# Layer 1's outputs and its feed forward in one set of pools, with one square root for four batches

## The chip, the cores and the metric

The kernel runs on one core of a Trainium2 chip. Its engines are PE (TensorE, matrix products and transposes), DVE (VectorE), ACT (ScalarE), POOL (GpSimd) and SP (SyncE, which issues the DMAs). Each engine takes its instructions in order; between engines they wait on semaphores. The metric is the device time of one execution in microseconds. Three executions of the kernel before took 2666.43, 2668.34 and 2669.78 us; the median is 2668.34.

## The reference, cut to what matters

The model is four layers of attention and feed forward on 4 x 1024 tokens of 128 features, each with a layer norm ahead and a residual sum behind. The change lies at the joint between layer 1's "attention" (a small network trained token by token, whose trained weights are then applied to all tokens) and layer 1's feed forward (eight experts with gates):

```python
def _layernorm(x, axis=-1, eps=1e-05):
    m = jnp.mean(x, axis=axis, keepdims=True)
    v = jnp.var(x, axis=axis, keepdims=True)
    return (x - m) / jnp.sqrt(v + eps)
...
    params, _ = jax.lax.scan(step, (W1, b1, W2, b2), (k, v))
    q = x @ W_Q
    return _mlp(params, q)                      # silu(q @ W1 + b1) @ W2 + b2
...
    gate_logits = jax.nn.softmax(x @ gate_w + gate_b, axis=-1)
    selected = (gate_logits >= THRESHOLD).astype(x.dtype)
    weights = gate_logits * selected
    wsum = jnp.sum(weights, axis=-1, keepdims=True)
    weights = weights / jnp.where(wsum == 0, jnp.ones_like(wsum), wsum)
    for e in range(E):
        out = out + weights[:, e:e + 1] * (x @ expert_w[e] + expert_b[e])
...
    x = x + _L1_attn_ref(_layernorm(x, axis=-1), ...)
    x = x + _L1_ffn_ref(_layernorm(x, axis=-1), ...)
    x = x + _L2_attn_ref(_layernorm(x, axis=-1), ...)
```

## The kernel before

All tokens stay in SBUF: `x` holds 32 tiles of 128 tokens by 128 features, four batches of eight tiles; `xnT` holds the normed tokens turned, features on the partitions. The layers run one after the other through one program; a scheduler orders the instructions of each engine by their dependencies and by the program's order, except in attention, which has an order written by hand. Tiles come from pools; a pool opened later is laid over the memory of one that has closed, and its tiles then wait until what was there is done with.

The stretch in question has these parts, in the program's order:

- `l1_attn` trains the small network (`l1_rounds`), and reads on every engine whether a slower path is to be taken (`tc.If`, line 681). Behind it opens the pools `l1o` and `l1q` and makes the outputs. First W_Q is turned and multiplied with W1 (`tp`, `wp`, `qw`), and the bias b2 is spread over the partitions (`b2p`, `bp`, `b2`). Then a loop of eight chunks of 512 tokens (lines 701 to 710): `hp`, one product with qw (L703); the Silu on ACT (L705); the bias added into x on POOL (`add_bias`, L169); `op`, four products with W2 (L709); and `op` added into x on DVE (`add_four`, L173). `hp` and `op` have two PSUM buffers each.
- `l1_ffn` opens its own pools: `ln` (f1l), `lps`, `one` (f1c), `two` (f1) and `ps`. It loads the experts' biases into `eb` with eight DMAs. Per batch it calls `ln_batch`, that is `ln_sums` (eight `bn_stats`, L134, and five small operations for sum and squares), `ln_moments` (the square root on ACT, L114, the reciprocal, and `nm`, L125) and `ln_scale` (xn on ACT, L154, and on POOL, L152, by turns; the transposes, L158; the copy into `xnT`, L164). `weights` makes the gates (L1014 and the small operations from L1019 to L1059), `biases` the weighted expert biases (L1065, L1070), `tile_of` the experts of one tile: two products of 512 columns (L1081, tile `ep`, three buffers), five multiply-adds on DVE (L1090), three scalings on ACT (L1088) and their sums on POOL (L1092).
- `l2_attn` begins with `layernorm(twice=...)`: the same steps with a second norm folded in, which takes more small operations for the root (lines 116 to 122, root at L123) and a scaled copy (L162). Its pool `ln` is laid over the memory in which f1l was. Attention's first products are L1205.

A function on ACT may need a table that is not loaded: the program then has an ACT_TABLE_LOAD ahead of it, at the same line. In the profile each f32 product shows as two matmul rows.

Of the kernel before, what the change touches and what calls it, by code (L numbers as in the profile page):

```python
# [27 lines left out]
class Net:  # L28
# [76 lines left out]
    def ln_moments(self, pool, b, twice=None):  # L105


        nc = self.nc
        if b not in self.ahead:
            self.ln_sums(pool, b)  # L110
        s, q = self.ahead.pop(b)
        rs = pool.tile([P, TPB], F32, tag="rs", name="rs")
        if twice is None:
            nc.scalar.activation(rs, q, AF.Sqrt, bias=self.eps, scale=1.0 / D)  # L114
# [12 lines left out]

    def ln_sums(self, pool, b):

        nc = self.nc  # L130

        st = pool.tile([P, TPB, 6], F32, tag="st", name="st")
        for i in range(TPB):
            nc.vector.bn_stats(st[:, i, :], self.x[:, b * TPB + i, :])  # L134
# [5 lines left out]
        nc.vector.tensor_add(q, q, d)  # L140
        nc.vector.tensor_add(s, st[:, :, 1], st[:, :, 4])
        self.ahead[b] = s, q
# [502 lines left out]
    def l1_attn(self):  # L645

        nc, tc = self.nc, self.tc
        wb1, wb2, wkv, wq = self.l1
        W1, B1 = wb1[:, 0:128], wb1[:, 128:129]
        W2, B2 = wb2[:, 0:128], wb2[:, 256:257]
        with ExitStack() as c_:
            one = c_.enter_context(tc.tile_pool(name="l1c", bufs=1))
            kT = one.tile([P, SEQ, NB], F32, tag="kT", name="kT")  # L660
            vT = one.tile([P, SEQ, NB], F32, tag="vT", name="vT")

            def project(bs, few, ln, lps, ps):
                by = [self.ln_moments(few, b) for b in bs]
                for b, m in zip(bs, by):
                    self.ln_scale(ln, lps, b, m)
                    for s in range(0, SEQ, 512):
                        for dst, cols in ((kT, slice(0, 128)), (vT, slice(128, 256))):
                            pp = ps.tile([P, 512], F32, tag="pp", name="pp")
                            nc.tensor.matmul(  # L670
                                pp, lhsT=wkv[:, cols], rhs=self.tok(b * TPB + s // P, 512), start=True, stop=True
                            )
                            if dst is kT:
                                nc.vector.tensor_copy(dst[:, s : s + 512, b], pp)
                            else:
                                nc.scalar.copy(dst[:, s : s + 512, b], pp)

            self.l0_ffn(project)
            bad = self.l1_rounds(one, kT, vT)
            many = nc.values_load(bad[0:1, 0:1], min_val=0, max_val=1)  # L680
            with tc.If(many > 0):
                self.l1_steps(kT, vT)
        with tc.tile_pool(name="l1o", bufs=2) as two, tc.tile_pool(name="l1q", bufs=2, space=PSUM) as ps:

            tp = ps.tile([P, D], F32, tag="one", name="tp", bufs=1)
            nc.tensor.transpose(tp, wq, self.ident)
            wqT = two.tile([P, D], F32, tag="wqT", name="wqT", bufs=1)
            nc.scalar.copy(wqT, tp)
            wp = ps.tile([P, D], F32, tag="one", name="wp", bufs=1)
            nc.tensor.matmul(wp, lhsT=wqT, rhs=W1, start=True, stop=True)  # L690
            qw = two.tile([P, D], F32, tag="qw", name="qw", bufs=1)
            nc.scalar.copy(qw, wp)
            b2p = ps.tile([1, D], F32, tag="two", name="b2p", bufs=1)
            nc.tensor.transpose(b2p, B2, self.ident)
            b2r = two.tile([1, D], F32, tag="b2r", name="b2r", bufs=1)
            nc.vector.tensor_copy(b2r, b2p)
            bp = ps.tile([P, D], F32, tag="two", name="bp", bufs=1)
            nc.tensor.matmul(bp, lhsT=self.ones[0:1, :], rhs=b2r, start=True, stop=True)
            b2 = two.tile([P, D], F32, tag="b2", name="b2", bufs=1)
            nc.vector.tensor_copy(b2, bp)  # L700
            for n in range(NB * SEQ // 512):
                hp = ps.tile([P, 512], F32, tag="hp", name="hp")
                nc.tensor.matmul(hp, lhsT=qw, rhs=self.tok(4 * n, 512), start=True, stop=True)  # L703
                a = two.tile([P, 512], F32, tag="a", name="a")
                nc.scalar.activation(a, hp, AF.Silu, bias=B1)  # L705
                self.add_bias(4 * n, b2)
                op = ps.tile([P, 4, D], F32, tag="op", name="op")
                for i in range(4):
                    nc.tensor.matmul(op[:, i, :], lhsT=a[:, i * P : (i + 1) * P], rhs=W2, start=True, stop=True)  # L709
                self.add_four(4 * n, op)  # L710

    def l1_rounds(self, keep, kT, vT):

# [316 lines left out]
    def l1_ffn(self):  # L1030


        nc, tc = self.nc, self.tc
        gw, gb, ew = self.f1
        E, OWN = 8, 5
        with ExitStack() as c:
            ln = c.enter_context(tc.tile_pool(name="f1l", bufs=2))
            lps = c.enter_context(tc.tile_pool(name="f1q", bufs=2, space=PSUM))
            one = c.enter_context(tc.tile_pool(name="f1c", bufs=2))
            two = c.enter_context(tc.tile_pool(name="f1", bufs=3))  # L1040
# [5 lines left out]
            ps = c.enter_context(tc.tile_pool(name="f1p", bufs=2, space=PSUM))  # L1046

            def weights(b):
                g = self.gates(one, ps, gw, gb, b * TPB, TPB)
                sel = one.tile([P, TPB, E], F32, tag="sel", name="sel")  # L1050
                nc.vector.tensor_scalar(sel, g, 0.1, None, ALU.is_ge)
                nc.vector.tensor_mul(g, g, sel)
                sm = one.tile([P, TPB], F32, tag="sm", name="sm")
                nc.vector.tensor_reduce(sm, g, axis=AX.X, op=ALU.add)
                z = one.tile([P, TPB], F32, tag="z", name="z")
                nc.vector.tensor_scalar(z, sm, 0.0, None, ALU.is_equal)
                nc.vector.tensor_add(sm, sm, z)
# [33 lines left out]
                for e in range(OWN, E):  # L1091
                    nc.gpsimd.tensor_add(xs, xs, sc[:, e - OWN, :])  # L1092

            self.ln_batch(ln, lps, 0)
            g = weights(0)
            for b in range(NB):
                if b + 1 < NB:
                    self.ln_batch(ln, lps, b + 1)
                biases(b, g)
                for i in range(TPB):  # L1100
                    tile_of(b * TPB + i, g[:, i, :])
                    if i == TPB // 2 and b + 1 < NB:
                        ahead = weights(b + 1)
                g = ahead
# [721 lines left out]
```

## Time and profile before

| what | us |
|---|---|
| median of three executions | 2668.34 |
| the profiled execution | 2665.29 |
| its span | 2663.6 |
| PE busy in the span | 2417.5 (91%) |
| DVE busy | 1795.2 (67%) |
| ACT busy | 1501.7 (56%) |
| POOL busy | 293.0 (11%) |
| outputs of layer 1, from the first `hp` to the last sum into x | 822.90 to 841.10 |
| feed forward of layer 1, to the last multiply on DVE | 841.10 to 945.70 |
| from there to attention's first product (L1205) | 945.70 to 956.30 |

The page of a profile has the busy time of each engine, the span in 40 slices with the clock that PE was granted, the DMA queues, the chain of waits that ended last, and the costliest groups of instructions. The timeline lists instructions by start, with duration, engine, line, operation, output and inputs, how many in a row ("x4"), and in brackets how long the engine had been idle and what released it. The windows give each engine's busy time in stretches. PEld is PE's loading of weights, which runs beside its products. Almost all DMA traffic of the stretch is the load of `eb`.

### The profile page before, as it was taken

The page shows a single profiled execution, that of the slowest core. Times are in us where ns is not written, and L with a number is a line of the kernel's source. Part 1 is how long each engine was busy: PE and PEld are TensorE (multiplying, and loading weights), DVE is VectorE, ACT ScalarE, POOL GpSimd, SP SyncE. Part 2 cuts the span into 40 slices and gives each one's busy share as a digit, 9 for nine tenths or more (in the row PEclk, how much of TensorE's full clock was granted, in tenths as well). Part 3 has the DMA queues.
Part 4 walks back from the last instruction along what each step waited for, and adds up shares of the span by engine and source line. Part 5 has one row for each costly group of instructions (what it writes and reads, how often), then busy time and mean ns, then how long its engine had stood idle before and what let it go on. Part 6 is the DMA issues. An engine that isn't in the chain of part 4 may idle for free.

```text
span 2663.6 us, 51041 instructions
## 1 busy us (share of the span) xinstructions
PE 2417.5 (91%) x19913; PEld 1222.1 (46%) x19913; DVE 1795.2 (67%) x3670; ACT 1501.7 (56%) x3333; POOL 293.0 (11%) x525
## 2 busy tenths in 40 slices
PE   5687758899997979999999779999999999999968
PEld 3455535699995333333333443333333333333356
DVE  5888877476764767776774357767767776777233
ACT  4466468455554434665566635666666566666632
POOL 6012021000002530000000440000000000000011
PEclk8699879899997989999999879999999999999969
DMA  1333320000000001001000000000000000000000
GB/s 45 74 77 74 73 74 1 1 1 1 1 1 2 1 9 18 14 15 18 14 14 6 5 5 10 9 10 8 8 9 12 8 9 10 8 8 8 3 18 18
DMA packets 116719, 46.66 MB, mean 18 GB/s; under 512 B 88473, under 2 KB 111097, under 8 KB 116474
## 3 DMA queue, kind: packets, MB, share of 16 engines
q1 hardware_dynamic: 116474, 43.35, 8.2%
q8 instruction: 159, 2.61, 0.4%
q14 instruction: 86, 0.70, 0.1%
HBM read 17.04 MB, written 12.98 MB: 11 GB/s over the span
## 4 chain that ended last, share of the span: by engine, by line
PE 57%; DVE 4%; ACT 1%; POOL 1%; issue 1%; SPq 0%; DMA 0%; POOLq 0%; DVEq 0%; ACTq 0%
PE pb L1319 32%; PE po L1341 16%; PE pa L1265 2%; DVE bm L1277 1%; PE pp L1205 1%; PE pv L1186 1%; DVE bm L1304 1%; PE tp L158 1%; PE gp L1014 1%; PE rp L1743 1%; DVE bm L1308 0%; PE pr L1598 0%; PE rp L1520 0%; PE ph L1756 0%; POOL sg L1753 0%
## 5 line engine op out<-in xcount | busy, mean ns | idle before, releaser
L1323 ACT ACTIVATE es<-pb 128x512 f32<-128x512 f32 x1536 | 836.3, 594 | 536.1 <-PE pb L1319 381.8
L1319 PE MATMUL pb<-q,k 32*128 32x512 f32 x3072 | 956.5, 641 | 3.9 <-DVE bm L1308 1.7
L1265 PE MATMUL pa<-k,q 32*128 32x512 f32 x2944 | 846.0, 650 | 10.4 <-DMA q<-q 10.3
L1277 DVE TENSOR_REDUCE bm<-pa 128x2 f32<-128x1024 f32 x496 | 605.0, 1225 | 261.1 <-PE pb L1319 168.0
L1341 PE MATMUL po<-es,v 128*32 128x256 f32 (+1 forms) x5760 | 480.0, 405 | 0.0
L1319 PEld LDWEIGHTS pb<-q,k 32*128 32x128 f32 x3072 | 313.5, 183 | 350.7 <-ACT es L1323 189.8
L1341 PEld LDWEIGHTS po<-es,v 128*32 128x32 f32 x5760 | 114.2, 108 | 543.1 <-issue 508.2
L1273 DVE TENSOR_REDUCE bm<-pa 128x16 f32<-128x1024 f32 x240 | 293.2, 1222 | 97.3 <-PE pb L1319 60.7
L1265 PEld LDWEIGHTS pa<-k,q 32*128 32x128 f32 x2944 | 234.4, 186 | 37.0 <-issue 18.6
L152 POOL TENSOR_SCALAR xn<-x,rs,nm 128x128 f32<-128x128 f32 x112 | 50.3, 464 | 1204.6 <-DVE nm L125 1026.9
L366 DVE TENSOR_TENSOR pr<-T,L 128x31 f32<-128x31 f32 (+15 forms) x248 | 92.0, 371 | 28.0 <-DMA L<-ld 20.7
L369 DVE TENSOR_TENSOR T<-T,pr 128x31 f32<-128x31 f32 (+15 forms) x248 | 93.1, 375 | 8.5
L1348 DVE COPY oT<-po 128x512 f32<-128x512 f32 x48 | 32.8, 682 | 95.6 <-PE po L1341 95.6
L158 PE MATMUL tp<-ident,xn 128*128 128x128 f32 x224 | 47.0, 361 | 42.7 <-ACT xn L154 38.1
L821 ACT ACTIVATE w<-tr,half 128x128 f32<-128x128 f32 x128 | 47.1, 368 | 48.3 <-PE tr L819 45.6
L796 ACT ACTIVATE a<-hp,wb 128x128 f32<-128x128 f32 x128 | 47.1, 368 | 41.6 <-PE hp L792 40.1
L1081 PE MATMUL ep<-L_ffn_expert_w,xnT 128*128 128x512 f32 x128 | 66.8, 654 | 3.3 <-DVE x L1090 3.1
L324 PE MATMUL wide<-bt,kt 32*128 32x128 f32 x512 | 29.9, 360 | 43.9 <-DVE mt L413 31.7
L486 PE MATMUL sp<-ux,kn 128*128 128x256 f32 x128 | 46.1, 493 | 17.7 <-ACT ux L475 17.7
L158 PEld LDWEIGHTS tp<-ident,xn 128*128 128x128 f32 x224 | 33.9, 179 | 61.2 <-ACT xn L154 47.0
L804 DVE TENSOR_TENSOR dlt<-gr,mask 128x128 f32<-128x128 f32 x96 | 28.0, 292 | 48.3 <-PE gr L802 48.3
L853 ACT COPY dr<-tr 128x128 f32<-128x128 f32 x128 | 34.1, 266 | 43.1 <-PE tr L851 41.1
(466 smaller groups left out, 3598.8 us busy)
## 6 DMA issues: line engine op xcount, KB each, us to landing
ld<-kk SPq DMA_DIRECT2D x128, 32.0 KB
L<-ld SPq DMA_DIRECT2D x8, 512.0 KB
td<-T SPq DMA_DIRECT2D x8, 512.0 KB
tb<-td SPq DMA_DIRECT2D x128, 32.0 KB
md<-nt SPq DMA_DIRECT2D x192, 2.0 KB
q<-md SPq DMA_DIRECT2D x192, 2.0 KB
x<-in_L_attn_x_dram SPq DMA_DIRECT2D x4, 512.0 KB
od<-o SPq DMA_DIRECT2D x32, 64.0 KB
```

Of the source, the lines that this page charges most:

```text
L152: nc.gpsimd.tensor_scalar(xn[:, i, :], src[:, i, :], sl, bl, ALU.mult, ALU.add)
L158: nc.tensor.transpose(tp[:, i, :], xn[:, 4 * n + i, :], self.ident)
L366: nc.vector.tensor_mul(pv, T[:, 0 : j + 1, j : j + 1].to_broadcast(sh), L[:, j : j + 1, j + 1 :].to_broadcast(sh))
L369: nc.vector.tensor_sub(T[:, 0 : j + 1, j + 1 :], T[:, 0 : j + 1, j + 1 :], pv)
L796: nc.scalar.activation(self.a, self.hp, AF.Silu, bias=B1)
L1081: nc.tensor.matmul(ep.rearrange("p a b -> p (a b)"), lhsT=self.tok(t), rhs=ew[:, 4 * h : 4 * h + 4, :].rearrange("p a b -> p (a b)"), star ...
L1265: nc.tensor.matmul(pa[:, j % 2, :], lhsT=st["q"][r, i * P : (i + 1) * P], rhs=st["k"][r, n * 512 : (n + 1) * 512], start=True, stop=True,)
L1273: nc.vector.tensor_reduce(out[:, :, 1:9], pa.rearrange("p j (c s) -> p j c s", c=8), axis=AX.X, op=ALU.max)
L1277: nc.vector.tensor_reduce(out[:, :, n : n + 1], pa, axis=AX.X, op=ALU.max)
L1319: nc.tensor.matmul(pb, lhsT=st["k"][r, kc * P : (kc + 1) * P], rhs=st["q"][r, n * 512 : (n + 1) * 512], start=True, stop=True,)
L1323: nc.scalar.activation(es[turn][:, j, :], pb, AF.Exp, scale=scale)
L1341: nc.tensor.matmul(po[r, cols], lhsT=vring[b % 2][:, kc, 4 * g + j, :], rhs=es[:, j, cols], start=kc == 0, stop=True, skip_group_check=True,)
```

## The change

The outputs leave `l1_attn` and become `l1_out`, called inside `l1_ffn` with that function's pools. It returns a function that makes the two chunks of one batch. `l1_ffn` calls it batch by batch and puts `ln_sums` of the batch behind each. Then `ln_roots` takes one square root, one reciprocal and one `nm` over all 32 columns, and the batches are scaled from slices of these. `rs` and `nm` come from f1c instead of f1l. In PSUM `hp` and `op` share the tag `ep`, which has three buffers; the small products use the tags `gp`, `ap` and `bp`. The three copies of the setup run on DVE; two of them ran on ACT.

```diff
+    def ln_roots(self, pool, bs):
+        nc = self.nc
+        for b in bs:
+            if b not in self.ahead:
+                self.ln_sums(pool, b)
+        for b in bs:
+            del self.ahead[b]
+        rs, nm = (pool.tile([P, len(bs), TPB], F32, tag=f"{t}{len(bs)}", name=t) for t in ("rs", "nm"))
+        own = slice(bs[0], bs[-1] + 1)
+        nc.scalar.activation(rs, self.sums[:, 1, own, :], AF.Sqrt, bias=self.eps, scale=1.0 / D)
+        nc.vector.reciprocal(rs, rs)
+        nc.vector.scalar_tensor_tensor(nm, self.sums[:, 0, own, :], -0.5, rs, ALU.mult, ALU.mult)
+        return [(rs[:, i, :], nm[:, i, :]) for i in range(len(bs))]
...
-        with tc.tile_pool(name="l1o", bufs=2) as two, tc.tile_pool(name="l1q", bufs=2, space=PSUM) as ps:
-            tp = ps.tile([P, D], F32, tag="one", name="tp", bufs=1)
-            nc.tensor.transpose(tp, wq, self.ident)
-            wqT = two.tile([P, D], F32, tag="wqT", name="wqT", bufs=1)
-            nc.scalar.copy(wqT, tp)
...
-            nc.scalar.copy(qw, wp)
...
-            for n in range(NB * SEQ // 512):
-                hp = ps.tile([P, 512], F32, tag="hp", name="hp")
...
-                op = ps.tile([P, 4, D], F32, tag="op", name="op")
...
+    def l1_out(self, one, two, ps):
...
+        def turned(tag, src, shape):
+            tp = ps.tile(shape, F32, tag=tag, name="tp", bufs=1)
+            nc.tensor.transpose(tp, src, self.ident)
+            t = one.tile(shape, F32, tag="t" + tag, name="t" + tag, bufs=1)
+            nc.vector.tensor_copy(t, tp)
+            return t
+
+        wqT = turned("gp", wq, [P, D])
+        b2r = turned("bp", B2, [1, D])
+        wp = ps.tile([P, D], F32, tag="ap", name="wp", bufs=1)
+        nc.tensor.matmul(wp, lhsT=wqT, rhs=W1, start=True, stop=True)
...
+        def batch(b):
+            for n in (2 * b, 2 * b + 1):
+                hp = ps.tile([P, 512], F32, tag="ep", name="hp", bufs=3)
                 nc.tensor.matmul(hp, lhsT=qw, rhs=self.tok(4 * n, 512), start=True, stop=True)
-                a = two.tile([P, 512], F32, tag="a", name="a")
+                a = two.tile([P, 512], F32, tag="a", name="a", bufs=2)
                 nc.scalar.activation(a, hp, AF.Silu, bias=B1)
                 self.add_bias(4 * n, b2)
+                op = ps.tile([P, 4, D], F32, tag="ep", name="op", bufs=3)
                 for i in range(4):
                     nc.tensor.matmul(op[:, i, :], lhsT=a[:, i * P : (i + 1) * P], rhs=W2, start=True, stop=True)
                 self.add_four(4 * n, op)
+        return batch
...
-            self.ln_batch(ln, lps, 0)
+            out = self.l1_out(one, two, ps)
+            for b in range(NB):
+                out(b)
+                self.ln_sums(ln, b)
+            by = self.ln_roots(one, range(NB))
+            self.ln_scale(ln, lps, 0, by[0])
             g = weights(0)
             for b in range(NB):
                 if b + 1 < NB:
-                    self.ln_batch(ln, lps, b + 1)
+                    self.ln_scale(ln, lps, b + 1, by[b + 1])
```

More of the change, by code (lines that the diff above doesn't have):

```diff
@@ L654, in l1_attn @@
         nc, tc = self.nc, self.tc
-        wb1, wb2, wkv, wq = self.l1
-        W1, B1 = wb1[:, 0:128], wb1[:, 128:129]
-        W2, B2 = wb2[:, 0:128], wb2[:, 256:257]
+        wkv = self.l1[2]
         with ExitStack() as c_:
@@ L682, in l1_attn @@
                 self.l1_steps(kT, vT)
-        with tc.tile_pool(name="l1o", bufs=2) as two, tc.tile_pool(name="l1q", bufs=2, space=PSUM) as ps:
-            tp = ps.tile([P, D], F32, tag="one", name="tp", bufs=1)
-            nc.tensor.transpose(tp, wq, self.ident)
-            wqT = two.tile([P, D], F32, tag="wqT", name="wqT", bufs=1)
-            nc.scalar.copy(wqT, tp)
-            wp = ps.tile([P, D], F32, tag="one", name="wp", bufs=1)
-            nc.tensor.matmul(wp, lhsT=wqT, rhs=W1, start=True, stop=True)
-            qw = two.tile([P, D], F32, tag="qw", name="qw", bufs=1)
-            nc.scalar.copy(qw, wp)
[L693 to L700, printed above, removed]
-            for n in range(NB * SEQ // 512):
-                hp = ps.tile([P, 512], F32, tag="hp", name="hp")
@@ new lines, in l1_out @@
+    def l1_out(self, one, two, ps):
+        nc = self.nc
+        wb1, wb2, _, wq = self.l1
+        W1, B1 = wb1[:, 0:128], wb1[:, 128:129]
+        W2, B2 = wb2[:, 0:128], wb2[:, 256:257]
+        def turned(tag, src, shape):
[8 more added lines that the diff above has]
+        nc.tensor.matmul(wp, lhsT=wqT, rhs=W1, start=True, stop=True)
+        qw = one.tile([P, D], F32, tag="qw", name="qw", bufs=1)
+        nc.vector.tensor_copy(qw, wp)
+        bp = ps.tile([P, D], F32, tag="gp", name="bp", bufs=1)
+        nc.tensor.matmul(bp, lhsT=self.ones[0:1, :], rhs=b2r, start=True, stop=True)
+        b2 = one.tile([P, D], F32, tag="b2", name="b2", bufs=1)
+        nc.vector.tensor_copy(b2, bp)
+        def batch(b):
+            for n in (2 * b, 2 * b + 1):
+                hp = ps.tile([P, 512], F32, tag="ep", name="hp", bufs=3)
```

## The prediction

> **What bounds the kernel now.** I read the slices first, then the windows by stage, then the timeline of the stage that the change touches. The page's chain of waits gives 57% to PE and 32% of it to the scores of attention (L1319), which the change leaves alone; it cannot be followed back beyond 980 us, so the stage in question, 816 to 956 us, has to be read from its timeline.
>
> ```profile
> PE   5687758899997979999999779999999999999968
> ...
> PEclk8699879899997989999999879999999999999969
> ```
>
> Slices are 66.6 us wide. Layer 1's outputs and feed forward lie in slices 13 to 15, where PE shows 7, 9 and 7 tenths and its clock 7, 9 and 8. By stage (columns: span; PE, weight load, DVE, ACT, POOL busy; granted clock; DMA):
>
> ```profile
> 822.90:841.10 18.20, 17.38 (x81) 11.13 (x80) 5.85 (x10) 6.54 (x9) 9.87 (x8) 0.87 0.00 1
> 841.10:846.30 5.20, 0.02 (x1) 0.03 (x1) 5.20 (x36) 2.43 (x5) 0.40 (x1) 0.85 0.00 2
> 846.30:852.40 6.10, 6.08 (x28) 5.45 (x29) 3.25 (x21) 4.87 (x11) 3.49 (x8) 0.50 0.00 0
> ...
> 865.30:876.00 10.70, 10.70 (x24) 5.52 (x23) 5.59 (x21) 5.26 (x12) 4.42 (x10) 0.53 0.00 1
> 876.00:945.70 69.70, 64.27 (x162) 24.84 (x160) 59.19 (x238) 34.08 (x109) 42.99 (x95) 1.00 0.00 1
> 945.70:956.30 10.60, 5.87 (x33) 4.32 (x33) 4.14 (x23) 9.29 (x18) 5.63 (x14) 0.73 0.01 2
> ```
>
> The reader is to see: the outputs run PE nearly full (17.38 of 18.20); then PE stands still for 5.2 us while DVE makes the moments; then it works 30 us at half clock; then the experts' tiles run PE-bound with DVE close behind; then a tail of 10.6 us belongs to layer 2's layer norm, with ACT busiest. The output loop and the moments in detail:
>
> ```profile
> 828.87 1.88 PE L703 MATMUL hp<-xnT,qw 128*128 128x512 f32 x4
> 829.99 0.69 ACT L705 ACTIVATE a<-hp,wb 128x512 f32<-128x512 f32 x1 [2.50 <-PE hp L703]
> 830.73 2.05 PE L709 MATMUL op<-wb,a 128*128 128x128 f32 x16
> 832.62 1.88 PE L703 MATMUL hp<-xnT,qw 128*128 128x512 f32 x4
> ...
> 840.39 0.69 DVE L173 TENSOR_TENSOR x<-op,x 128x512 f32<-128x512 f32 x1 [0.20 <-PE op L709]
> 841.00 1.83 DVE L134 BATCH_NORM_STATS2 st<-x 128x6 f32<-128x128 f32 x9
> 843.51 1.28 ACT L114 ACT_TABLE_LOAD   x1 [4.47 <-DVE sums L140]
> 845.73 2.04 ACT L154 ACTIVATE xn<-x,nm,rs 128x128 f32<-128x128 f32 x5
> ```
>
> A matmul in f32 is two rows, so "x4" at 828.87 is two hp matmuls in a row: PE makes the second while ACT takes the Silu of the first. One turn of 3.75 us (828.87 to 832.62) serves two chunks of 512 tokens.
>
> **Part by part.** The built program of the changed kernel lists each engine's order; I use it for places, the profile for durations.
>
> *The output loop.* The changed order on PE is hp, four op, hp, four op, eight times over; in before it is two hp, eight op. PE is in order, so hp of chunk n+1 stands behind op of chunk n, which waits for the Silu of n. At full clock from the rows: Silu starts 1.12 us after hp (829.99-828.87), op 1.86 after (830.73), four op take half of 832.62-830.73, 0.945; period 2.81 against 3.75/2 = 1.875. At half clock: Silu 2.11 after hp (822.99 to 825.10), op's weights 2.85 after (825.84), eight rows at 0.236 (the 16 cold rows of pv, 3.78 us at 981.89) 1.89; period 4.74. Once more: the changed order puts the Silu's table load, 1.28 us, behind the wait for the first hp; in before it is done at 823.9, under hp. That is paid in full. DVE's add and four moments per chunk (0.69 and 4 x 0.203, from nine in 1.83) and POOL's bias adds (1.23 each) lie inside 2.81.
>
> How many chunks run cold? Before, the clock rose at about 827.6, as the 2 us windows show. Its changes here (844.7, 858.4, 861.8, 875.4) lie 3.41 us apart or multiples of it. **Here a rule is weighed.** The Trainium skill ("TensorE: Matmul & The Clock Gate", Part 1) has the clock released after one busy window of about 3.4 us and taken back after an idle one; gaps under 3 us should not matter. By it, one cold chunk: 4.74 + 1.28 from 822.99 to 829.0, seven warm to 848.7, against 840.28 for the last op in before: +8.4. But in this trace windows in which PE is shown 100% busy did not release it (848.1 to 851.5 and 851.5 to 854.9 stayed at 0.50, with transposes and 8-column gates in them), while 854.9 to 858.3, all 512-column rows, did. A cold turn has a gap of about 1 us in 4.74, so I take two cold chunks: second hp at 829.0, third at 833.75, six warm turns to 850.6: **+10.3**. Ends: +8.4, and never released: 829.0 + 7 x 4.74 = 862.2, +21.9.
>
> *Moments behind the outputs, one root.* Before, from last op (840.28) to the first transpose (846.28): 6.0. Changed: add 0.72 until the next can start (840.39 to 841.00, and 0.11), last four moments 0.81, five small operations 0.62 (947.64 to 948.26), root of 128x32 about 0.35 (0.30 for 128x8), reciprocal 0.25, nm 0.22, first xn and transpose 0.58: 3.55. The root's table load now stands ahead of its wait, behind the last Silu, so it is hidden. **-2.4**; ends -3 and -1.5. The gap still leaves the array cold behind it, as in before.
>
> **Second rule.** "ScalarE: Activation LUTs" (Table sets: the hidden batching unit) tells to batch functions by set and puts a switch at 2.66 us, load and drain. The stretch goes from nine loads to four. By the rule -13.3. By the rows a load is 1.283 us, and of the five that go only that at 843.51 is on the path (counted above); those at 856.02, 857.63 and 866.26 lie beside PE at 100% and half clock, that at 891.10 beside PE with matmuls queued. I take nothing more.
>
> *Front of the feed forward (846 to 876).* PE-bound at half clock; the order is the same up to the gates of batch 1. Then batch 3's eight transposes (0.27 each cold) and four gate groups (eight rows at 0.12) come in, 3.1, less the 1.4 us that PE waited at 860.3: +1.8 by the seventh expert matmul, booked in the next item. Cover gone: if the clock rose earlier here it would be a gain; see rivals.
>
> *Tiles.* Layer 2's moments leave DVE's queue here, and PE no longer waits for DVE (0.3 to 0.74 us before every fourth matmul from 898 on). From 876 on: 57 expert matmuls x 0.925 (3.70 for four at 884.94) 52.7, six bias matmuls x 1.05 6.3, last gates 0.96, turns 0.5, last tile on DVE 1.75, and the 1.8: 64.0 against 69.65 (876.0 to the last multiply's end, 945.65). -5.6; I take **-5**, since DVE and POOL keep their 1.3 and 1.52 us per tile. Ends -7 and -1.
>
> *The tail.* This is the part that the diff doesn't tell. In before 26 of layer 2's 32 moments stand among the tiles. In the changed order all 32 stand behind the last multiply on DVE, the root behind ACT's last scaling, POOL's xn behind its last add: rs and nm left the pool f1l, so layer 2's pool reaches 128 bytes into eb. Now, for before:
>
> ```profile
> 945.64 0.28 DVE L134 BATCH_NORM_STATS2 st<-x 128x6 f32<-128x128 f32 x1
> ...
> 949.75 1.64 ACT L154 ACTIVATE xn<-x,nm,rs 128x128 f32<-128x128 f32 x4
> ...
> 954.61 1.63 ACT L162 ACTIVATE xnT<-tp,L_attn_beta,L_attn_gamma 128x512 f32<-128x512 f32 x2
> ...
> 956.30 3.78 PE L1205 MATMUL pp<-xnT,L_attn_Wk 128*128 128x512 f32 x4 [0.87 <-ACT xnT L162]
> ```
>
> Changed, from the last multiply: nine moments 1.83, sums with one moment 0.58, seven moments and six root steps 1.98, the load 1.28 (waits for these sums in the built order) and root; nm of batch 0 in its place on DVE at 6.5. Then ACT is the chain: xn 1.65 and two turned copies about 1.5 for batch 0 and for 1, roots between: xn of batch 2 at 13.4. From there as in before, 949.75 to 956.30, 6.55: 20.0 against 10.65 (945.65 to 956.30): **+9.3**; ends +7.5 and +12. SP's queue keeps its order; no DMA moves.
>
> Sum: 10.3 - 2.4 - 5 + 9.3 = +12.2. The profiled execution took 2665.29 (span 2663.6 and 1.7 around it), so 2677.5; the runs' median, 2668.34, lies 3.05 above it: **2680.5**.
>
> **Rivals.** (a) *The clock is never released in the outputs*: +21.9 for 10.3, 2692. For it: the gap in each turn. Against: full 512-column rows are there. 13%. (b) *Faster*: the shorter gap before the first transpose, 3.55 for 6.0, falls across two clock windows and the array stays at full clock through 846 to 876. Its price: half of the 11.51 + 4.14 + 7.11 + 6.62 us that experts, biases, gates and transposes take there, 14.7 less what ACT and DVE then bound, say 13. With the loop at +8.4: 8.4 - 2.4 - 13 - 5 + 9.3 = -2.7, 2665.6. It decides from 10.3 us saved there. Against: at 861.8 the clock fell although PE was 0.6 busy in the window ahead. 7%. (c) *The tail doesn't come* (layer 2's moments find gaps, or ACT's copies run closer): +2 for 9.3, 2673. The built order speaks against it. 8%. (d) *The tiles don't quicken*, since POOL's chain of adds or the three ep buffers hold PE at 2.15 us a tile: 2685.5. 10%. The forecast: 62%.
>
> **Numbers.** The range takes in the ends of each item without the sum of all worst ones: 2667 to 2694. A measurement of this kernel tells 0.2%, 5.3 us, from no change. Slower by more: forecast, a, d, and most of the ends, 0.85; within: c and the low ends, 0.09; faster: b, 0.06.
>
> **What would show it.** Right: hp and op alternate on PE with Silu gaps near 0.9 us and a loop of 26 to 29 us for 17.3; first transpose 3 to 4 us behind the last op; the tile stage near 64 us with PE at 95%; all 32 layer 2 moments behind the last multiply and about 20 us to L1205's first matmul. Wrong: a loop under 22 us, moments of layer 2 among the tiles, or a clock of 1.00 between the outputs and the tiles.

## The result, and the profile after

| | before | after |
|---|---|---|
| median of eight executions each | 2667.79 us | 2678.53 us |
| range of the executions | 2665.61 to 2674.61 | 2674.32 to 2690.05 |
| ratio, 95% interval | | 1.0044, 1.0028 to 1.0060 |
| span of the profiled execution | 2663.6 us | 2672.5 us |

The change makes the kernel 0.44% slower. The slices of the page show little of it: in slice 15 PE is 6 tenths for 7 before and its clock 7 for 8, in slice 16 the clock is 8 for 9. Ten microseconds are a sixth of a slice. One of the 14 executions of a kernel below (the one with one root on the moments' own pool) took 3303.5 us at a clock of 0.63, and is left out of its ratio.

```profile
PE   5687758899997969999999779999999999999968
...
PEclk8799879899997978999999879999999999999968
```

The windows show it. They are laid from event to event here, so that they can be held against other kernels (columns as before: span; PE, weight load, DVE, ACT, POOL busy; granted clock; DMA). After:

```profile
818.81:845.85 27.04, 19.12 (x81) 10.82 (x80) 12.98 (x51) 7.98 (x10) 9.81 (x8) 0.85 0.00 1
845.85:849.74 3.89, 0.00 (x0) 0.00 (x1) 2.68 (x12) 0.95 (x4) 0.47 (x2) 0.70 0.00 0
849.74:856.50 6.76, 6.72 (x29) 6.06 (x30) 0.35 (x2) 5.47 (x11) 4.71 (x11) 0.50 0.00 0
...
876.90:944.04 67.14, 61.51 (x146) 23.30 (x144) 53.16 (x179) 27.03 (x93) 39.66 (x88) 1.00 0.00 1
944.04:963.31 19.27, 8.14 (x33) 5.44 (x33) 11.89 (x81) 14.22 (x29) 9.08 (x21) 0.56 0.01 2
```

The reader is to see four things. The outputs take 27.04 us with PE busy for 19.12, so PE waits inside the loop. It then stands still 3.89 us behind the last `op`. The array starts cold (0.50). And behind the last multiply a tail of 19.27 us has DVE and ACT busier than PE. From the same events in both traces (before: first `hp` 822.99, last `op` ends 840.28, first transpose 846.28, last multiply ends 945.65, L1205 956.30):

| stage | before | after | difference | predicted |
|---|---|---|---|---|
| output loop, first `hp` to the end of the last `op` | 17.29 | 27.04 | +9.75 | +10.3 |
| from there to the first transpose | 6.00 | 3.89 | -2.11 | -2.4 |
| front and tiles, to the end of the last multiply | 99.37 | 94.30 | -5.07 | -5 |
| tail, to attention's first product | 10.65 | 19.27 | +8.62 | +9.3 |
| stretch, with the setup of 2.25 and 2.28 in front | 135.56 | 146.78 | +11.2 | +12.2 |

What lies outside the stretch is the same code, and it scatters: attention's first product is 1707.3 us before the end of the span in before and 1709.2 in after, and the stretch began at 820.74 and 816.53. Over the profiles of the kernels below, its start lies between 816.5 and 828.5. A single time can therefore not show one microsecond of the change; the stretch can, and it repeats: 146.76 us for 146.78 in a second profile of the changed kernel.

The loop in the timeline of after:

```profile
818.81 2.08 PE L726 MATMUL hp<-xnT,qw 128*128 128x512 f32 x2
...
820.95 1.28 ACT L728 ACT_TABLE_LOAD   x1 [12.37 <-PE hp L726]
822.25 0.69 ACT L728 ACTIVATE a<-hp,wb 128x512 f32<-128x512 f32 x1
822.99 2.08 PE L732 MATMUL op<-wb,a 128*128 128x128 f32 x8 [2.10 <-ACT a L728]
824.85 1.91 PE L726 MATMUL hp<-xnT,qw 128*128 128x512 f32 x2
...
827.55 1.16 PE L732 MATMUL op<-wb,a 128*128 128x128 f32 x8 [0.78 <-ACT a L728]
828.54 1.02 PE L726 MATMUL hp<-xnT,qw 128*128 128x512 f32 x2
...
830.40 1.16 PE L732 MATMUL op<-wb,a 128*128 128x128 f32 x8 [0.84 <-ACT a L728]
```

"x2" is one `hp`: no second one follows it. In brackets PE waits for the Silu before every `op`, 0.78 to 0.84 us from the second chunk on. In the first chunk it waits 2.10, since the table load (1.28) stands behind the wait for `hp` (820.95). The clock comes up between `hp` (1.91 for two rows at 824.85) and `op` of the second chunk (1.16 for eight rows, 2.08 when cold): one and a half cold chunks.

PE's rows among the tiles, four products (eight rows) for two tiles, first of before and then of after:

```profile
932.74 3.85 PE L1081 MATMUL ep<-L_ffn_expert_w,xnT 128*128 128x512 f32 x8 [0.30 <-DVE x L1090]
936.89 3.94 PE L1081 MATMUL ep<-L_ffn_expert_w,xnT 128*128 128x512 f32 x8 [0.30 <-DVE x L1090]
...
933.52 3.67 PE L1106 MATMUL ep<-L_ffn_expert_w,xnT 128*128 128x512 f32 x8 [0.35 <-DVE x L1115]
937.55 3.67 PE L1106 MATMUL ep<-L_ffn_expert_w,xnT 128*128 128x512 f32 x8 [0.35 <-DVE x L1115]
```

Two tiles take 4.03 us for 4.15 before. PE waits for DVE in both, 0.35 us for 0.30: with layer 2's moments gone from the tiles, DVE is still close behind PE.

The tail in the timeline of after:

```profile
944.15 1.84 DVE L149 BATCH_NORM_STATS2 st<-x 128x6 f32<-128x128 f32 x9
...
948.23 1.28 ACT L123 ACT_TABLE_LOAD   x1 [4.58 <-issue]
...
950.05 1.65 ACT L169 ACTIVATE xn<-x,nm,rs 128x128 f32<-128x128 f32 x4 [0.32 <-DVE nm L125]
...
956.71 1.65 ACT L169 ACTIVATE xn<-x,nm,rs 128x128 f32<-128x128 f32 x4
...
963.31 2.07 PE L1235 MATMUL pp<-xnT,L_attn_Wk 128*128 128x512 f32 x2 [0.87 <-ACT xnT L177]
```

Every moment of layer 2 is behind the last multiply (944.04). DVE begins them 0.11 us after it, with no wait: they stand there in DVE's order. It is not a wait for `eb` on the chip, since the last product that reads `eb` ended at 925.5. The table load is waited for; then ACT scales batch after batch, and the `xn` at 956.71 stands where the one at 949.75 stood before.

### The profile page after: what moved, and what is told of

Its sections match the earlier page's. It is cut to its first block, busy times and chain, and to the rows that moved or that the text cites. A ratio compares the mean times of both kernels' runs of the same rounds, so it can differ in the third digit from the quotient of the medians.

```text
span 2672.5 us, 51023 instructions
## 1 busy us (share of the span) xinstructions
PE 2414.3 (90%) x19913; PEld 1218.6 (46%) x19913; DVE 1795.9 (67%) x3666; ACT 1493.2 (56%) x3323; POOL 292.1 (11%) x525
## 4 chain that ended last, share of the span: by engine, by line
PE 56%; DVE 4%; ACT 1%; POOL 1%; issue 1%; SPq 0%; DMA 0%; POOLq 0%; DVEq 0%; ACTq 0%
PE pb L1349 32%; PE po L1371 16%; PE pa L1295 2%; DVE bm L1307 1%; PE pp L1235 1%; DVE bm L1334 1%; PE pv L1216 1%; PE gp L1039 1%; PE rp L1773 1%; PE tp L173 1%; DVE bm L1338 0%; PE pr L1628 0%; PE kp L1541 0%; PE ph L1786 0%; DVE m L1537 0%
## 5 line engine op out<-in xcount | busy, mean ns | idle before, releaser
L1295 PE MATMUL pa<-k,q 32*128 32x512 f32 x2944 | 846.2, 650 | 10.1 <-DMA q<-q 10.1
L501 PE MATMUL sp<-ux,kn 128*128 128x256 f32 x128 | 46.2, 495 | 18.1 <-ACT ux L490 18.1
L1115 DVE SCALAR_TENSOR_TENSOR x<-ep,g,x 128x128 f32<-128x128 f32 x160 | 50.3, 345 | 16.4 <-ACT sc L1113 14.4
```

The costliest lines, as they stand in the source:

```text
L1115: nc.vector.scalar_tensor_tensor(xs, eps[e // 4][:, e % 4, :], g[:, e : e + 1], xs, ALU.mult, ALU.add)
L1295: nc.tensor.matmul(pa[:, j % 2, :], lhsT=st["q"][r, i * P : (i + 1) * P], rhs=st["k"][r, n * 512 : (n + 1) * 512], start=True, stop=True,)
```

## The experiments

The theory at this point: the loop is long because `hp` and `op` alternate; the tail is long because rs and nm left the pool f1l, so that layer 2's pool reaches into `eb`; the tiles are shorter only because layer 2's moments left them. All expectations below were written before their run. "Stretch" is from the turn of W_Q to attention's first product, from each profile.

| kernel | loop | to first transpose | front and tiles | tail | stretch | ratio to before, 95% interval |
|---|---|---|---|---|---|---|
| after, second profile | 27.04 | 3.90 | 94.27 | 19.27 | 146.76 | 1.0051 (1.0034 to 1.0067) |
| after, pairs | 17.62 | 5.23 | 90.99 | 19.27 | 135.39 | 1.0014 (1.0001 to 1.0027) |
| after, rs and nm back in f1l | 27.04 | 3.90 | 98.86 | 10.66 | 142.74 | 1.0056 (1.0036 to 1.0077) |
| the same, second run | 27.03 | 3.90 | 98.89 | 10.46 | 142.56 | 1.0039 (1.0023 to 1.0054) |
| after, both edits | 17.88 | 4.96 | 98.73 | 10.11 | 133.96 | 0.9996 (0.9985 to 1.0006) |
| after, a root for each batch | 31.48 | 0 | 84.86 | 19.27 | 137.88 | 1.0011 (1.0001 to 1.0021) |
| before, alternating | 27.48 | 5.99 | 99.29 | 10.65 | 145.66 | 1.0037 (1.0023 to 1.0051) |
| before, moments in f1c | 20.19 | 0.97 | 91.32 | 19.22 | 133.95 | 1.0001 (0.9992 to 1.0010) |
| before, moments in a pool of their own | 20.20 | 0.97 | 92.88 | 10.44 | 126.74 | 0.9975 (0.9965 to 0.9984) |
| the same, second run | 20.20 | 0.97 | 92.84 | 10.42 | 126.68 | 0.9982 (0.9973 to 0.9992) |
| the same, with one root | 17.35 | 5.60 | 95.84 | 10.10 | 131.14 | 1.0003 (0.9993 to 1.0013) |
| after, pairs, own pool, two roots | 19.03 | 0 | 97.42 | 10.66 | 129.39 | 0.9987 (0.9978 to 0.9995) |

**Pairs on PE again.**

```diff
-                hp = ps.tile([P, 512], F32, tag="ep", name="hp", bufs=3)
+                hp = lps.tile([P, 512], F32, tag="tp", name="hp")
...
```

> The changed kernel with one edit: hp takes its PSUM buffers from the transposes' pool (two buffers) and no longer shares the three of ep with op, so that PE's order is again two hp, eight op. Theory (the alternation of hp and op on PE makes the loop longer): from the first hp to the last op's end about 18 us for 27.0; the exposed table load now lies under the second hp; some 8 to 9.5 us less than the changed kernel, ratio to before 1.0005 to 1.0015. Rival (the loop is long because the clock is late or because the Silu's table load and the setup on DVE are exposed, not because of the order): at most 2 us less, ratio 1.0035 or more, loop 25 us or more.

The loop went from 27.04 to 17.62 us with the setup still on DVE: the alternation is the loop's cost, and the rival fell. The stretch lost 11.4 us, two more than the loop gave, for the clock was 1.00 from 866.5 us on in this profile (0.84 and 0.66 in after, as far behind the first transposes) although the first transposes were at 0.50. Front and tiles were 3.3 us shorter for it, and the gap 1.3 us longer.

**The pool of rs and nm.**

```diff
-            by = self.ln_roots(one, range(NB))
+            by = self.ln_roots(ln, range(NB))
```

> The changed kernel with one edit: rs and nm of the one root come from the layer norm's pool again, so that layer 2's layer norm no longer reaches into eb. Theory (those 128 bytes push layer 2's moments behind the last multiply, and the tiles are shorter only because the moments left them): moments of layer 2 stand among the tiles again; from the last multiply to attention's first product about 11 us for 19.3, while the tile stage takes back 3 to 5 us; 4 to 5.5 us less than the changed kernel in all, ratio 1.002 to 1.003. Rival A (the tail has another cause than the overlap): no change, ratio 1.0040 or more. Rival B (the tiles are shorter for another reason and stay so): 8.5 us less, ratio 1.0012 or less.

> The changed kernel with rs and nm back in the layer norm's pool, once more, beside the changed kernel itself in the same call: in the profiles of these two the stretch from the turn of W_Q to attention's first product is 4 us shorter with the edit (142.7 for 146.8), but the time over six executions was not. Theory (the stretch is shorter by 4 us, and executions differ by where the clock's windows fall, which the edit does not touch): the medians of the two stand 1 to 7 us apart in favour of the edit. Rival (the edit has a cost outside this stretch, or makes the cold phases likelier): medians equal or the edit slower, and a second profile shows the time elsewhere.

In both profiles the tail is back (10.66 and 10.46 us) and front and tiles take 4.6 us back, as the theory had it: 4.0 and 4.2 us off the stretch. The time did not show it in the first run (1.0056, where 1.002 to 1.003 was expected). In the second run the median was 2675.17 us, and beside it that of the unchanged changed kernel was 2680.08, so the two stood 4.9 us apart, within the 1 to 7 expected; but the intervals of the two ratios overlap. So the mechanism and its size in the stretch are shown, and the gain in time is not.

What the moments of layer 2 cost in the tiles depends on their place in DVE's order. Here are two of them in this kernel, and two in before:

```profile
882.87 0.29 DVE L149 BATCH_NORM_STATS2 st<-x 128x6 f32<-128x128 f32 x1 [0.99 <-POOL x L1117]
885.94 0.29 DVE L149 BATCH_NORM_STATS2 st<-x 128x6 f32<-128x128 f32 x1 [0.98 <-POOL x L1117]
...
899.46 0.28 DVE L134 BATCH_NORM_STATS2 st<-x 128x6 f32<-128x128 f32 x1
900.00 0.28 DVE L134 BATCH_NORM_STATS2 st<-x 128x6 f32<-128x128 f32 x1
```

In this kernel eight moments, seven of them the first ones, stand so close behind the tile that they read that DVE waits for it, mostly for POOL's last sum: 6.6 us in all, beginning at 879.9. In before the first comes at 897.2 and none waits. The same divides the other kernels in which these moments stand among the tiles: with one or two roots DVE waits eight times (6.1 to 6.7 us), with a root for each batch not once.

> The changed kernel as it is. It is run for a second profile and for its times on the chip on which the edit above is run. Expected: ratio 1.003 to 1.0055; its outputs again have one and a half cold chunks (27 us from the first hp to the last op's end) if the phase of the clock's windows against the work is the same in every execution; if the phase is free, another profile shows another number of cold chunks, between 24 us (one) and 40 us (all).

The outputs again had one and a half cold chunks, and so had both profiles with rs and nm back in f1l (loops of 27.04 and 27.03 us). Four profiles are few, but they give no sign of a free phase.

**Both edits together.**

> Both edits together. Theory: they lie in different stages and add up: some 13 to 15 us less than the changed kernel, ratio 0.998 to 0.9995, a little faster than before, by what the one root with the moments behind the outputs brings (about 2 us). Rival (the parts overlap, or the moments' gain is lost once the loop is short, since DVE's moments then come after it): ratio 1.000 to 1.002.

The two add up in the stretch: 12.8 us less than after, a little under the 13 to 15 expected, and 1.6 less than before. In time that is no difference from before. With one root and pairs the gap is 4.96 us, for DVE's moments no longer keep up with the shorter loop; the gap's gain over before is 1.0 us, not 2.

**Each part alone, on the kernel before.** `hp` and `op` with one tag of three buffers:

```diff
-                hp = ps.tile([P, 512], F32, tag="hp", name="hp")
+                hp = ps.tile([P, 512], F32, tag="hop", name="hp", bufs=3)
...
-                op = ps.tile([P, 4, D], F32, tag="op", name="op")
+                op = ps.tile([P, 4, D], F32, tag="hop", name="op", bufs=3)
```

> The kernel before with one edit: hp and op share one PSUM tag of three buffers in the pool that they have, so that hp and op alternate on PE as in the changed kernel. Theory (the alternation alone makes the loop longer): from the turn of W_Q to attention's first product about 143 to 145 us for the 135.6 of before; period 2.8 warm for 1.875; the table load is hidden here, so 1.3 us less than the loop of the changed kernel; ratio to before 1.0025 to 1.004. Rival (it takes the other parts of the change, setup on DVE, moments on DVE between the adds, to make the loop long): within 3 us of before, ratio below 1.0015.

```profile
833.62 2.08 PE L709 MATMUL op<-wb,a 128*128 128x128 f32 x8 [0.78 <-ACT a L705]
...
838.18 2.08 PE L709 MATMUL op<-wb,a 128*128 128x128 f32 x8 [0.78 <-ACT a L705]
...
842.80 1.16 PE L709 MATMUL op<-wb,a 128*128 128x128 f32 x8 [0.84 <-ACT a L705]
...
845.65 1.16 PE L709 MATMUL op<-wb,a 128*128 128x128 f32 x8 [0.84 <-ACT a L705]
```

One shared tag alone gives the whole loop of the change: 27.48 us, +10.1 in the stretch, ratio 1.0037. The smaller expectation in it fell: with the table load hidden under `hp` the loop should have been 1.3 us shorter than the changed one. It was not, since the clock came up only in the third chunk here. The rows give both parts: PE's first wait for a Silu is 0.78 us for 2.10 in after, so the exposed load does cost 1.3 us there; and one more chunk ran cold here (4.56 us from `op` to `op` for 2.85 warm), which is 1.7.

The moments in f1c:

```diff
-            self.ln_batch(ln, lps, 0)
+            self.ln_scale(ln, lps, 0, self.ln_moments(one, 0))
...
-                    self.ln_batch(ln, lps, b + 1)
+                    self.ln_scale(ln, lps, b + 1, self.ln_moments(one, b + 1))
```

> The kernel before with one edit: rs and nm of the feed forward's layer norm come from f1c, so that layer 2's pool reaches 128 bytes into eb. Theory: the moments of layer 2 stand behind the last multiply, the tail is 8 to 9.5 us longer and the tiles 4 to 5 us shorter, from the turn of W_Q to attention's first product about 139.5 for 135.6, ratio 1.001 to 1.002. Rival A (the overlap of pools does nothing): 135.6, ratio within 0.0005 of 1. Rival B (the tiles stay as long as they were): 144 us, ratio 1.003 or more.

The tail came as expected, 19.22 us. The stretch did not: 133.95 us for 139.5. The edit passes its pool on to `ln_sums`, so st and d moved along with rs and nm. In before these lie over the memory of the outputs' pool, and in the built program all moments stand behind the outputs; in f1c they lie over nothing that is in use, and the moments of batches 0 to 2 run among the outputs. The windows of this kernel:

```profile
844.39:845.36 0.97, 0.00 (x1) 0.03 (x1) 0.97 (x4) 0.85 (x3) 0.70 (x2) 1.00 0.00 0
845.36:852.20 6.84, 6.84 (x41) 4.99 (x42) 4.21 (x21) 6.28 (x14) 2.75 (x7) 1.00 0.01 2
...
936.68:955.90 19.22, 8.14 (x33) 5.47 (x33) 11.91 (x82) 14.22 (x29) 9.06 (x21) 0.56 0.01 2
```

PE stands 0.97 us instead of 6.0, and the array then works at full clock (1.00) where the kernels above had 0.50. The rows are not the same: six of 512 columns stand among the transposes and gates here, where after has these only from 855.93 on. This is the mechanism of the prediction's rival (b), at a gap a quarter as long.

**The root batch by batch, on the changed kernel.**

```diff
-            by = self.ln_roots(one, range(NB))
-            self.ln_scale(ln, lps, 0, by[0])
+            self.ln_scale(ln, lps, 0, self.ln_moments(one, 0))
...
-                    self.ln_scale(ln, lps, b + 1, by[b + 1])
+                    self.ln_scale(ln, lps, b + 1, self.ln_moments(one, b + 1))
```

> The changed kernel with the one root undone: each batch has its own root again, taken from f1c (so the overlap with eb stays). In the built order batch 0's normed tokens, transposes and gates then stand among the outputs of batches 2 and 3, at the price of seven table loads for Silu and root in turn. Theory (one root saves table loads but holds every transpose behind the last output): the loads, 6 of 1.28 us inside the loop, cost 4 to 7 us of the loop, the transposes and gates moved into its gaps and the moments' gap of 3.9 us give 6 to 10 back: 0 to 4 us less than the changed kernel, ratio 1.003 to 1.0045. Rival (the one root is what carries the change): 4 us or more slower than the changed kernel, ratio 1.006 or more.

Both theories missed: 8.9 us less in the stretch, where 0 to 4 less or at least 4 more were expected. The loop grew by 4.4 us with transposes, gates and six more table loads in it, but the work that followed no longer met a cold array (1.00 in the 6.8 us behind the loop), and the gap was gone. The one root is not a gain of the change that the other parts hid; in this order it is a loss.

**A pool for the moments alone, on the kernel before.** A pool f1s between f1l and f1c takes st, d, rs and nm, so that neither the outputs' tiles nor `eb` is touched:

```diff
             ln = c.enter_context(tc.tile_pool(name="f1l", bufs=2))
+            few = c.enter_context(tc.tile_pool(name="f1s", bufs=2))
...
-            self.ln_batch(ln, lps, 0)
+            self.ln_scale(ln, lps, 0, self.ln_moments(few, 0))
...
-                    self.ln_batch(ln, lps, b + 1)
+                    self.ln_scale(ln, lps, b + 1, self.ln_moments(few, b + 1))
```

> The kernel before with one edit: the moments (st, d, rs, nm) of layer 1's feed forward have a small pool of their own, which lies over nothing that the outputs use and which keeps layer 2's pool away from eb. Theory (in before the moments wait for the outputs only because their memory lies under the outputs' tiles, and the tail comes only from the overlap with eb): the moments of batches 0 to 2 run among the outputs, first transpose 1 us behind the last op for 6.0 at 3 us more in the loop for the table loads of the roots; tail 10.7 to 11.5 us; from the turn of W_Q to attention's first product 128 to 131 us for 135.6, ratio 0.9970 to 0.9985. Rival (what the front wins is lost again in the tiles, which are bound by PE and DVE alike): 133 us or more, ratio 0.999 or more.

> The faster kernel once more, for a second profile beside the run with one root. Expected: ratio 0.9965 to 0.9985; the clock again at full speed in the transposes behind the last op, if that comes from the short gap and not from one lucky execution; else 0.50 there and a stretch of 132 us or more.

This beats both kernels: 2659.69 us beside 2666.83 for before, and 2661.96 beside 2667.73 in the second run. From the kernel with the moments in f1c it differs only in the pool, and loop and gap are the same (20.20 and 0.97 us). So the two show what the overlap of layer 2's pool with f1c costs by itself: 8.8 us in the tail, of which front and tiles give 1.6 back, 7.2 us in the stretch. Its windows:

```profile
822.83:843.03 20.20, 17.20 (x81) 11.00 (x80) 13.76 (x52) 11.96 (x15) 9.86 (x8) 0.89 0.00 1
843.03:844.00 0.97, 0.01 (x1) 0.04 (x1) 0.97 (x4) 0.85 (x3) 0.71 (x2) 1.00 0.00 0
844.00:850.80 6.80, 6.80 (x41) 4.95 (x41) 4.24 (x21) 6.24 (x14) 2.78 (x7) 1.00 0.01 2
...
936.88:947.32 10.44, 5.58 (x33) 4.07 (x33) 4.74 (x27) 9.08 (x18) 5.67 (x14) 0.81 0.01 2
```

**One root on this kernel**, the headline of the change by itself:

```diff
-            self.ln_scale(ln, lps, 0, self.ln_moments(few, 0))
+            by = self.ln_roots(few, range(NB))
+            self.ln_scale(ln, lps, 0, by[0])
...
-                    self.ln_scale(ln, lps, b + 1, self.ln_moments(few, b + 1))
+                    self.ln_scale(ln, lps, b + 1, by[b + 1])
```

> The faster kernel (moments of layer 1's feed forward in their own pool, outputs in pairs, roots batch by batch) with one edit: one root for all four batches, as in the change. It prices the one root alone. Theory (one root saves two pairs of table loads in the loop, 2.5 us of waiting PE, but makes PE stand about 5 us behind the last op, and the array then goes through the transposes and gates at half clock): loop 17.5 for 20.2, gap 5 for 1.0, clock 0.50 in the 7 us behind it, from the turn of W_Q to attention's first product 132.5 to 134.5 us for 126.7, ratio 0.999 to 1.0005. Rival (the one root is worth its saved loads, and the gain came from the pool alone): 124 to 127 us, ratio 0.9975 or less.

```profile
827.48:844.83 17.35, 17.35 (x81) 11.19 (x80) 12.05 (x43) 7.67 (x10) 9.86 (x8) 0.86 0.01 2
844.83:850.43 5.60, 0.00 (x2) 0.00 (x1) 4.37 (x22) 0.93 (x4) 0.46 (x2) 0.90 0.00 0
850.43:857.20 6.77, 6.73 (x29) 6.05 (x30) 0.37 (x2) 5.47 (x11) 4.70 (x11) 0.50 0.00 0
```

PE is never idle in this loop (17.35 of 17.35), and the two pairs of loads cost 2.85 us in the kernel with four roots. But PE then stands 5.60 us (4.6 more), and the stretch is 4.4 us longer, ratio 1.0003 for 0.9975 and 0.9982. The clock came back earlier than expected behind it, so the stretch is 131.14 us and not 132.5 to 134.5; the rival is far off. The array is back at 0.50 as the theory had it, but that is not where the time goes. To the end of the seventh expert product and behind it, with four roots and then with one:

```profile
844.00:869.97 25.97, 23.64 (x94) 15.02 (x94) 13.25 (x57) 17.12 (x38) 8.67 (x21) 0.74 0.00 1
869.97:936.88 66.91, 62.76 (x152) 23.80 (x150) 59.54 (x235) 34.30 (x108) 43.32 (x96) 1.00 0.00 1
...
850.43:874.37 23.94, 22.70 (x100) 15.46 (x100) 9.64 (x41) 14.46 (x36) 8.74 (x21) 0.81 0.00 1
874.37:946.26 71.89, 63.40 (x145) 22.75 (x144) 61.51 (x246) 33.82 (x106) 43.35 (x96) 1.00 0.00 1
```

With one root the first part is 2.0 us shorter, since the clock is at half there for 9.1 us and with four roots, where it falls later, for 13.7. The tiles are 5.0 us longer: layer 2's moments come earlier with one root, and eight of them make DVE wait 6.7 us. So the price of the one root is the standstill and the tiles, and not, on balance, the cold array. That the waits are the whole of the 5.0 us is argued from the rows; no run has the one root without them.

**Two roots**, on the changed kernel with pairs and the pool of its own:

```diff
...
-                self.ln_sums(ln, b)
-            by = self.ln_roots(one, range(NB))
+                self.ln_sums(few, b)
+                if b == 1:
+                    by = self.ln_roots(few, (0, 1))
+            by += self.ln_roots(few, (2, 3))
```

> The changed kernel with hp in the transposes' pool (pairs on PE), the moments in a small pool of their own, and two roots in place of one: batches 0 and 1 behind the outputs of batch 1, batches 2 and 3 behind the last output. Theory (one root over all four holds the first transposes behind the last moments): one pair of table loads more in the loop, 1.3 to 2.6 us, but the first transpose 1 us behind the last op for 5.0; from the turn of W_Q to attention's first product 130 to 132.5 us, ratio 0.9978 to 0.9992, less than with both edits and one root (133.96). Rival (the number of roots does not matter, since the transposes run at half clock either way): 133.5 us or more.

129.39 us, a little better than expected, between one root (131.14, with before's setup) and four (126.7). Its transposes followed the last `op` without a gap, at 1.00.

## Why the prediction was right, and where not

The forecast was 2680.5 us; the median was 2678.53. Each term of the sum was of the right sign and within 0.7 us. Three were right for the reasons given; the third below, front and tiles, was right by luck.

- *The output loop, +10.3.* Measured +9.75. The alternation alone was shown to be enough (before with one shared tag, +10.1 in the stretch) and its removal to take all but 0.3 us of it (17.62 us). The term has two small errors: one and a half cold chunks, not two, and a warm period of 2.855 us, not 2.81. Neither the rule (one) nor the rows (two) had the number of cold chunks; before with one tag had more than two.
- *Moments and one root, -2.4.* Measured -2.11. The items are there in order: load hidden behind the last Silu, root 0.32, reciprocal 0.35 (0.25 assumed), nm 0.19. What the step left out is that the one root has a price which the sum of this change hid: "the gap still leaves the array cold" was taken as given, and as soon as the rest of the stretch allowed a gap of 1 us, the one root cost 4.4 us, net of the saved loads: 4.6 in the gap and 5.0 in the tiles, and nothing, on balance, for the cold array.
- *Tiles and front, -5.* Measured -5.07, by two errors that cancel. The end of the seventh expert product is the point at which the forecast divided the two. Ahead of it and behind it, first in before and then in after:

```profile
846.28:876.38 30.10, 28.33 (x86) 17.21 (x86) 14.11 (x67) 17.70 (x39) 9.71 (x22) 0.57 0.00 1
876.38:945.65 69.27, 63.89 (x161) 24.68 (x160) 59.14 (x238) 33.70 (x108) 42.94 (x95) 1.00 0.00 1
...
849.74:877.08 27.34, 26.82 (x101) 17.36 (x101) 10.22 (x42) 14.51 (x36) 9.15 (x21) 0.67 0.00 1
877.08:944.04 66.96, 61.33 (x146) 23.25 (x144) 53.14 (x178) 26.85 (x93) 39.48 (x88) 1.00 0.00 1
```

The forecast had +1.8 ahead of this point and some -7 behind it; it came to -2.8 and -2.3. Ahead, "PE-bound at half clock" is the step that failed: PE had 15 rows more to do there and was still quicker, since the clock was at half for 18.1 us instead of 25.7 (0.67 on average for 0.57). Behind, "PE no longer waits for DVE" failed: its waits for DVE were eight of 3.4 us together in before and ten of 4.3 in after, its share is 92% in both and not 95%, and the stage took 67.0 us where the forecast had 62 to 64. Some 1.9 of the 2.3 us are transposes and gates that moved ahead of the point, so the tiles themselves gained about 0.4. This is no accident of one execution: the second profile of after has 27.26 and 67.01 us, and before with one shared tag 30.08 and 69.22. In the changed kernel the moments do cost the tiles time when they return (71.64 us for 66.96 behind the point, 27.22 for 27.34 ahead), but there eight of them make DVE wait, and in before none does. So moving rs and nm spared the tiles a cost that the one root would have brought, and not one that before had. Why the clock was kept longer in the front stays open.
- *The tail, +9.3.* Measured +8.62, with the first `nm` 5.8 us behind the last multiply (949.87) for 6.5, and its cause shown from both sides: putting rs and nm back brings 10.66 us, moving them into f1c in before brings 19.22, and a pool of their own 10.44.
- *Rivals.* The clock came up in the outputs (not a). The tail came (not c). Front and tiles quickened together, but the tiles by little, so rival (d) was nearly right about them; DVE held them, and not POOL. Rival (b), the array at full clock behind the outputs, did not come at a gap of 3.89 us. At 0.97 us it came, in three profiles of two kernels, for 10.5 to 11.5 us from the first transpose on, and not through the whole front. Where between those it ends is not shown. The Trainium skill ("TensorE: Matmul & The Clock Gate", "Why this matters for your kernels") asks for no gap over some 3 us between bursts: behind the outputs the traces agree, with 0 and 0.97 us at 1.00 behind them and 3.89 to 6.0 us at 0.50. In the front they do not: the clock fell at 861.78 in before and at 867.87 in after, where PE's longest gap in the 4 us ahead was 1.41 and 0.48 us; there the measurement stands against the page. Its other page ("ScalarE: Activation LUTs", "Table sets: the hidden batching unit") would favour the one root for its fewer loads; by the runs, the two pairs of loads cost 2.85 us of the loop and the gap that replaces them costs more.

## What to carry to other kernels

When stages are merged into shared pools, look first at what now shares buffers and what lies over what: here one PSUM tag of three buffers, shared, undid a software pipeline of two chunks (+10 us; a shared tag with more buffers was not tried), and 128 bytes of overlap put the next layer's moments behind everything else (+9 us in the tail, of which the tiles gave half back in one kernel and a fifth in another), while the intended saving was 2 us. A sum that comes out right can hide two terms that are wrong: divide the measured stage where the forecast divided it. One operation batched over all data saves its fixed cost but makes all that follows wait for the last input; count the standstill of the matrix engine, and see where the work that comes free early lands in the orders of the other engines: an engine that takes its instructions in order waits for one that stands too early. And where executions scatter by more than the effect, measure from event to event in the trace, and repeat the profile.

## What the runs showed of the hardware that was not expected

In the front, how busy PE was did not decide whether the clock stayed. These are the windows at 1.00 up to the fall, one in before and then two in after, and the first two at 1.00 in the kernel with pairs:

```profile
858.36:861.78 3.42, 2.01 (x18) 1.81 (x16) 1.35 (x9) 0.81 (x2) 0.00 (x0) 1.00 0.00 0
...
861.04:864.46 3.42, 3.29 (x26) 2.73 (x24) 0.99 (x7) 0.25 (x2) 0.00 (x0) 1.00 0.00 0
864.46:867.87 3.41, 3.06 (x19) 2.21 (x20) 2.45 (x12) 3.21 (x11) 0.00 (x0) 1.00 0.00 0
...
861.81:865.22 3.41, 3.41 (x22) 2.45 (x21) 0.00 (x0) 2.13 (x5) 1.74 (x4) 1.00 0.00 0
865.22:868.64 3.42, 2.94 (x21) 2.19 (x20) 2.77 (x16) 2.27 (x8) 0.00 (x0) 1.00 0.00 0
```

In after PE was busy for 3.06 of 3.41 us, with transposes, gates and one bias product, and the clock fell. With pairs it was busy for 2.94 of 3.42 us with work of the same kinds, and the clock stayed at 1.00. What decides it is open.

Two executions of one kernel agree within 0.2 us over this stretch of 127 to 147 us, and differ by up to 5 us in its start, with the same code ahead. What makes the part ahead scatter was not looked into.
